# Where the edge features meet their weights: in the last attention loop, or in four earlier ones

## The chip, the cores and the metric

The kernel runs on one core of a Trainium2 chip as one program. The time is the device time of that core in microseconds (us), the median of ten runs. The engines are named as in the profile: PE (matrix products, with PEld for loading weights), DVE (vector work), ACT (activations and copies), POOL (here almost only indirect DMAs: gathers and scatters of rows by an index), SP (here only starts DMAs). Each engine works through its own instructions in order.

## The reference

A graph of 3125 nodes with 256 features each and 50,000 edges sorted by destination goes through four layers; each layer is an attention over the edges and then a feed-forward part, each added to `x`. The third feed-forward part holds an attention of its own over another graph of 65,536 edges. Only the fourth attention uses the edges' own features:

```python
x = x + L0_gnn(norm(x), edge_index, ...);  x = x + L0_ffn(norm(x), ...)
x = x + L1_gnn(norm(x), edge_index, ...);  x = x + L1_ffn(norm(x), ...)
x = x + L2_gnn(norm(x), edge_index, ...);  x = x + L2_ffn(norm(x), other_edges, ...)
x = x + L3_gnn(norm(x), edge_index, edge_attr_256, ...);  x = x + L3_ffn(norm(x), ...)

def L3_gnn(x, edge_index, edge_attr, Wq, bq, Wk, bk, Wv, bv, We, Ws, bs):
    q, k, v = x @ Wq + bq, x @ Wk + bk, x @ Wv + bv       # 8 heads of 32
    e = edge_attr @ We                                    # 50000 x 256 by 256 x 256
    kj = k[src] + e
    alpha = segment_softmax(einsum("ehc,ehc->eh", q[dst], kj) / sqrt(32), dst)
    out = segment_sum((v[src] + e) * alpha, dst)
    return out + (x @ Ws + bs)
```

`L2_gnn` is two attentions, one after the other, so the graph is walked five times: g0, g1, g2a, g2b and, with edge features, g3. The product `e` depends on two inputs only and on nothing that the layers compute.

## The kernel before

**Edges.** The edges are split into 128 runs, one per partition, of T = 391 edges each; column `t` of a table holds the t-th edge of every run. Loops go over columns in groups of GW = 8, so each attention loop has 49 groups, the last with 7 columns. If the edges are not sorted (`L.wrong` > 0, not the case for this input) a counting sort makes the table, and `gnn3` first gathers the features into order (lines 838 to 844).

**The loops g0, g1, g2a, g2b** (`gat_once`, lines 592 to 613). Per group, POOL makes 8 gathers of 128 rows each into the tile `hg` (4 buffers); DVE adds the logits (line 607), runs two scans for the running maximum (645, 646) and subtracts (649); ACT takes the exponential `e` (652) and copies the maxima (653); DVE multiplies by `e` into a PSUM tile `v` in two halves (660) and adds the running sums column by column (668); SP stores the group, 1088 KB, to `OUT` (611). The order of DVE and ACT is that of the program text inside these loops (`manual_schedule`); PE, POOL and SP are ordered by the planner.

**After each loop**, `join_chunks` joins the 128 runs: PE turns the maxima (`mRT`, line 724), DVE scans them (729, 730), PE turns them back (733, 734), ACT takes an exponential `rs_` (739), DVE scales `R` (740), PE multiplies it (`carried`, 742); meanwhile POOL gathers `fixrow` from the stored rows (721); then ACT takes a second exponential (748), DVE mends the row and SP stores it (754). Only then can `node_results` gather the nodes' rows (`ng`).

**The sort of the second graph** (`sort_keys`, lines 289 to 347) belongs to the time of g0's loop: 14 of its stages go from DVE to PE (transposes), an ACT copy and back to DVE. The planner puts it between the groups.

**The loop in `ffn2`** (lines 1377 to 1417) has 8 steps. Each makes 64 gathers of 96-byte rows on POOL, computes up to six expert units on PE and ACT (28 in all, line 1348 on), starts one eighth of a copy of all edge features to a DRAM tile `attr` (`copy_features`, line 960, 6.25 MB a step), and then does one step of attention on DVE and ACT; `hg` has 3 buffers. The expert units store their results `y` to DRAM, 512 KB each (1370).

**The last attention loop** (`gnn3`, lines 889 to 942). Per group, POOL makes 16 gathers (8 rows `kv`, 8 rows `q`, 3 buffers each), SP loads 1 MB of `attr` into `at` (902), and `project` turns each pair of columns on PE (907), copies it on ACT (909) and multiplies it by `We` on PE into the PSUM tile `ape` (913), two pairs ahead. DVE adds `ape` to the keys and the values and multiplies by the queries (930, 932, 933), sums over each head (937), and goes on as in the other loops. `ffn3` follows.

Of the kernel before, what the change touches and what calls it, by code (L numbers as in the profile page):

```python
# [9 lines left out]
F32 = mybir.dt.float32  # L10
# [9 lines left out]
P = 128  # L20
C = 256
KC = C // P
N = 3125
NT = 25
NP = NT * P
# [3 lines left out]
GB = 64  # L29
GV = 4  # L30
# [8 lines left out]
class Kernel:  # L39
# [514 lines left out]
    def gat_once(self, L, tag, load_z, load_w, a_src, a_dst, H, dh, eps, loops, use):  # L554
# [4 lines left out]
        nc, tc, T, Ep = self.nc, self.tc, L.T, L.Ep  # L559
        Fh = H * dh  # L560
        W = Fh + H
# [4 lines left out]
        with tc.tile_pool(name=tag + "k", bufs=1) as kp:  # L566
# [25 lines left out]
            with tc.tile_pool(name=tag + "e", bufs=1) as sp, tc.tile_pool(name=tag + "v", bufs=4) as vp, \  # L592
                    tc.tile_pool(name=tag + "vp", bufs=2, space=PSUM) as pp, \
                    tc.manual_schedule(engines={mybir.EngineType.DVE, mybir.EngineType.Activation}):

                ad = sp.tile([P, T, L.zc], F32, name="ad")
                self.spread(L, D, ad, H, tag)
                rows = OUT[:Ep].rearrange("(p t) w -> p t w", p=P)
                carry = None
                for t in range(0, T, GW):  # L600
                    n = min(GW, T - t)
                    g = vp.tile([P, GW, RW], F32, name="hg")
                    for j in range(n):
                        self.gather(g[:, j, :], HT, L.tab[:, t + j, 0:1])
                    l = vp.tile([P, H, GW + 1], F32, name="l")
                    ln = l[:, :, 1 : n + 1]
                    nc.vector.tensor_tensor(
                        ln, g[:, :n, W:].rearrange("p n h -> p h n"), ad[:, t : t + n, :H].rearrange("p n h -> p h n"), ALU.add)
                    self.lrelu(ln, ln)
                    carry = self.weigh(L, carry, vp, pp, t, n, l, g, H, dh)  # L610
                    nc.sync.dma_start(out=rows[:, t : t + n, :], in_=g[:, :n, :])
                nc.vector.tensor_copy(R, carry[0])
                nc.vector.tensor_copy(mR, carry[1][:, :, 0])  # L613

# [9 lines left out]
    def weigh(self, L, carry, vp, pp, t, n, l, g, H, dh):  # L624
# [201 lines left out]

    def gnn3(self, L):

        nc, tc, a, T, Ep = self.nc, self.tc, self.a, L.T, L.Ep
        H, dh = 8, 32  # L830
        W = C + H
        RW = W + H
        Q = self.dram.tile([NP, C], F32, name="g3_Q")
        KV = self.dram.tile([NP, C + W], F32, name="g3_KV")
        OUT = self.dram.tile([Ep + 1 + P, RW], F32, name="g3_OUT")
        heads = lambda x: x.rearrange("p n (h d) -> p n h d", h=H)
        r = nc.values_load(L.wrong[0:1, 0:1], min_val=0, max_val=P)
        with tc.If(r > 0):
            with tc.tile_pool(name="g3s", bufs=3) as sp:
                rows = self.attr.rearrange("(p t) c -> p t c", p=P)  # L840
                for t in range(T):
                    x = sp.tile([P, C], F32, name="ax")
                    self.gather(x, a["edge_attr_256"], L.tab[:, t, 2:3])
                    nc.sync.dma_start(out=rows[:, t, :], in_=x)
# [37 lines left out]
        with tc.tile_pool(name="g3k", bufs=1) as kp:  # L882
            R = kp.tile([P, W], F32, name="R")
            mR = kp.tile([P, H], F32, name="mR")
            we = kp.tile([P, KC, C], F32, name="we")
            nc.sync.dma_start(out=we, in_=a["L3_gnn_We"].rearrange("(k p) f -> p k f", p=P))
            attr = self.attr.rearrange("(p t) c -> p t c", p=P)
            rows = OUT[:Ep].rearrange("(p t) w -> p t w", p=P)
            with tc.tile_pool(name="g3v", bufs=3) as vp, tc.tile_pool(name="g3vp", bufs=1, space=PSUM) as pp, \
# [4 lines left out]
                def project(i):  # L894

                    if i >= len(pairs):
                        return
                    t, j = pairs[i]
                    n = min(GW, T - t)
                    if j == 0:  # L900
                        at[t] = vp.tile([P, GW, C], F32, name="at", bufs=2)
                        nc.sync.dma_start(out=at[t][:, :n, :], in_=attr[:, t : t + n, :])
                    k2 = min(2, n - j)
                    pt = pp.tile([P, 2, KC, P], F32, name="apt")
                    for i2 in range(k2):
                        for k in range(KC):
                            nc.tensor.transpose(pt[:, i2, k, :], at[t][:, j + i2, k * P : (k + 1) * P], self.ident)  # L907
                    aT = vp.tile([P, 2, KC, P], F32, name="aT")
                    nc.scalar.copy(aT[:, :k2], pt[:, :k2])  # L909
                    pe = pp.tile([P, 2, C], F32, name="ape", bufs=2)  # L910
                    for i2 in range(k2):
                        for k in range(KC):
                            nc.tensor.matmul(pe[:, i2, :], aT[:, i2, k, :], we[:, k, :], start=(k == 0), stop=(k == KC - 1))  # L913
                    proj[i] = pe

                project(0)
                project(1)
                carry, i = None, 0
                for t in range(0, T, GW):
                    n = min(GW, T - t)  # L920
# [5 lines left out]
                    for j in range(0, n, 2):  # L926
                        k2 = min(2, n - j)
                        pe = proj.pop(i)
                        kj = pp.tile([P, 2, C], F32, name="kj")
                        nc.vector.tensor_tensor(kj[:, :k2], g[:, j : j + k2, :C], pe[:, :k2], ALU.add)  # L930
# [10 lines left out]
                nc.vector.tensor_copy(R, carry[0])  # L941
                nc.vector.tensor_copy(mR, carry[1][:, :, 0])

            self.join_chunks(L, "g3", OUT, R, mR, H, dh)
# [5 lines left out]
            self.node_results(L, "g3", OUT, H, dh, 1e-16, None, use)  # L950

    def copy_features(self, E, i, n):

        nc, tc = self.nc, self.tc
        src = self.a["edge_attr_256"]
        assert E % 16 == 0
        cut = lambda x: x.rearrange("(s r) c -> s r c", s=16)
        size = E // 16
        lo, hi = size * i // n, size * (i + 1) // n
        tc.keep_in_program_order(nc.sync.dma_start(out=cut(self.attr[:E])[:, lo:hi], in_=cut(src[:E])[:, lo:hi]))  # L960
        if i == 0:
            nc.sync.dma_start(out=self.attr[E:], in_=src[: self.attr.shape[0] - E])

# [327 lines left out]
    def ffn2(self, L):  # L1291
# [12 lines left out]
        with tc.tile_pool(name="f2", bufs=1) as sp:  # L1304
# [35 lines left out]
            with tc.tile_pool(name="f2e", bufs=1) as ep, tc.tile_pool(name="f2v", bufs=3) as vp, \  # L1340
# [7 lines left out]
                def expert(e, b0, n):  # L1348
# [9 lines left out]
                    for f in range(FC):  # L1358
# [1 line left out]
                        for k in range(KC):  # L1360
                            nc.tensor.matmul(ps[:, :n], w1[:, k, f * P : (f + 1) * P], zT[:, k, b0 : b0 + n], start=(k == 0), stop=(k == KC - 1))
                        nc.scalar.activation(hT[:, f, :n], ps[:, :n], AF.Gelu, bias=b1[:, e * FC + f : e * FC + f + 1])
                    y = wp.tile([P, 4, C], F32, name="y")
                    for i in range(n // P):
                        po = pp.tile([P, C], F32, name="ps2")
                        for f in range(FC):
                            nc.tensor.matmul(po, hT[:, f, i * P : (i + 1) * P], w2[:, f, :], start=(f == 0), stop=False)
                        nc.tensor.matmul(po, ones, b2[:, e, :], start=False, stop=True)
                        nc.scalar.copy(y[:, i, :], po)
# [7 lines left out]
                for i, t in enumerate(range(0, T, GB)):  # L1377
# [134 lines left out]
def tile_kernel(ctx: ExitStack, tc: tile.TileContext, a, out):  # L1512
    k = Kernel(tc, ctx, a, out)
    k.attr = k.dram.tile([(50000 + P - 1) // P * P, C], F32, name="attr")
    A = k.edges_by_destination("A", a["src"], a["dst"], 50000, 8)

    with tc.tile_pool(name="s4", bufs=1) as k.sort_pool, tc.tile_pool(name="sortp", bufs=1, space=PSUM) as k.sort_psum:
        k.gnn0(A)
# [30 lines left out]
```

## Time and profile before

| | us |
|---|---|
| median of 10 runs | 6276.6 (6273.5 to 6282.3) |
| the profiled execution | 6279.5 |
| its span, first to last instruction | 6277.4 |

| part | from to | us |
|---|---|---|
| loop g0, first gather to `R` | 149.0 to 665.8 | 517 |
| loop g1, end at `R` | 1939.7 | |
| loop g2a, first gather to `R` | 2319.8 to 2821.9 | 502 |
| loop g2b, first gather to last `R` | 2934.8 to 3434.0 | 499 |
| loop of ffn2, first gather to last store | 3572.1 to 4342.7 | 771 |
| loop g3, first gather to `R` | 4556.7 to 5577.5 | 1021 |

Over the whole span DVE is busy 56%, POOL 51%, PE 41%, ACT 13%. A row of the profile's groups reads: line, engine, operation, output tile <- input tiles, number of instructions | busy us, mean ns of one | idle time of that engine just before them, and what ended it ("issue" is time in which it waited for nothing that the profile shows). A row of the timeline reads: start, duration, engine, line, operation, tiles, and in brackets the idle time before it and what ended it. A row of the windows gives the busy time and the number of instructions of PE, PEld, DVE, ACT and POOL in a stretch, then the granted clock of PE as a share of full speed, the mean busy share of the 16 DMA engines, and GB/s.

### The profile page before, as it was taken

The numbers are of one execution on the slowest core, as the hardware profiler recorded it, in microseconds if no ns is written. First come the engines' busy times: TensorE is split into PE (matmuls) and PEld (weight loads), VectorE is DVE, ScalarE is ACT, GpSimd is POOL, SyncE is SP. The second block draws the span as 40 slices with busy tenths as digits, with TensorE's granted clock in tenths as the row PEclk, the third lists the DMA queues.
The fourth block names the chain that finished last, engine by engine and source line by source line (L and its number), as shares of the span: only waits on it lengthen the run. The fifth ranks groups of instructions, "written<-read, shape, count | busy, mean of one in ns | idle before, by whom it ended". The sixth has DMA issues, their size and how long they took to land. (4 is left out here: it accounts for less than half of the span.)

```text
span 6277.4 us, 39477 instructions
## 1 busy us (share of the span) xinstructions
PE 2590.0 (41%) x9265; PEld 1740.5 (28%) x9265; DVE 3503.0 (56%) x8011; ACT 794.1 (13%) x1810; POOL 3224.6 (51%) x3326
## 2 busy tenths in 40 slices
PE   2000049921001930002000599400566666639999
PEld 1000037710000620001000355200245555525555
DVE  6998611156886268884776411112778888871111
ACT  1000012210001110001000122100011111102222
POOL 3777430037774137765776576675077777740000
PEclk9555569955555975555555699755776666657999
DMA  5566335516663026663666134522377887730000
GB/s 192 189 226 222 124 113 169 157 57 198 224 219 109 14 66 225 224 217 111 210 211 205 46 103 126 157 55 69 142 257 263 263 269 261 262 122 16 10 11 26
DMA packets 398594, 963.74 MB, mean 154 GB/s; under 512 B 92478, under 2 KB 241053, under 8 KB 365966
## 3 DMA queue, kind: packets, MB, share of 16 engines
q1 hardware_dynamic: 236254, 538.71, 24.0%
q0 software_dynamic: 162096, 422.40, 23.9%
q8 instruction: 77, 1.26, 0.1%
q14 instruction: 167, 1.37, 0.1%
HBM read 611.38 MB, written 400.71 MB: 161 GB/s over the span
## 5 line engine op out<-in xcount | busy, mean ns | idle before, releaser
L724 PE MATMUL mRT<-ident,mR 128*8 128x128 f32 (+2 forms) x6 | 2.2, 373 | 2222.3 <-DVE mR L613 1352.2
L129 POOL DMA_INDIRECT hg<-g_H,A_tab x782 | 758.0, 969 | 238.9 <-issue 226.4
L668 DVE SCALAR_TENSOR_TENSOR hg<-hg,A_keep,v 128x264 f32<-128x264 f32 (+1 forms) x1368 | 666.2, 487 | 44.2
L129 POOL DMA_INDIRECT hg<-f_H,B_tab x512 | 516.0, 1008 | 239.0 <-issue 147.5
L724 PEld LDWEIGHTS mRT<-ident,mR 128*8 128x8 f32 (+2 forms) x6 | 0.5, 82 | 2224.9 <-issue 2224.9
L913 PE MATMUL ape<-we,aT 128*128 128x256 f32 x1564 | 492.0, 485 | 149.9 <-DVE kv L932 146.3
L129 POOL DMA_INDIRECT kv<-g_KV,A_tab x391 | 369.8, 946 | 295.7 <-issue 281.9
L660 DVE TENSOR_TENSOR v<-hg,e 128x1056 f32<-128x1056 f32 (+1 forms) x392 | 487.8, 1244 | 3.5 <-ACT e L652 3.5
L913 PEld LDWEIGHTS ape<-we,aT 128*128 128x128 f32 x1564 | 382.9, 251 | 249.5 <-DVE kv L932 163.3
L129 POOL DMA_INDIRECT hg<-g2a_H,A_tab x391 | 371.9, 951 | 119.1 <-issue 107.3
L129 POOL DMA_INDIRECT q<-g_Q,A_tab x391 | 369.7, 946 | 122.6 <-issue 105.7
L129 POOL DMA_INDIRECT hg<-g2b_H,A_tab x391 | 369.7, 945 | 119.1 <-issue 111.8
L1501 DVE SCALAR_TENSOR_TENSOR xs<-ps,g,xs 128x256 f32<-128x256 f32 x200 | 94.2, 484 | 457.4 <-PE ps L1500 457.4
L1386 DVE TENSOR_TENSOR l<-hg,ad 128x256 f32<-128x256 f32 x8 | 6.3, 790 | 610.1 <-DMA hg<-f_H,B_tab 610.1
L652 ACT ACTIVATE e<-d 128x72 f32<-128x72 f32 (+1 forms) x245 | 54.8, 224 | 2135.4 <-DVE d L649 2135.3
L125 PE MATMUL tr<-ident,z 128*128 128x128 f32 x450 | 111.0, 378 | 499.5 <-DVE z L117 435.8
L134 POOL DMA_INDIRECT A_Z<-D,A_first x100 | 99.2, 992 | 354.8 <-PE tr L125 316.2
L907 PE MATMUL apt<-ident,at 128*128 128x128 f32 x782 | 195.1, 385 | 197.7 <-ACT aT L909 189.1
L129 POOL DMA_INDIRECT y<-f_Y,pos x50 | 47.4, 948 | 397.6 <-DMA f_Y<-y 382.6
L125 PEld LDWEIGHTS tr<-ident,z 128*128 128x128 f32 x450 | 72.6, 203 | 537.0 <-ACT ln_rs L109 316.4
L1494 ACT ACTIVATE hT<-ps,bn 128x512 f32<-128x512 f32 (+1 forms) x224 | 162.4, 731 | 389.7 <-PE ps L1492 389.7
L930 DVE TENSOR_TENSOR kj<-kv,ape 128x512 f32<-128x512 f32 x196 | 135.8, 693 | 132.6 <-PE ape L913 117.4
(476 smaller groups left out, 6481.8 us busy)
## 6 DMA issues: line engine op xcount, KB each, us to landing
g_OUT<-hg SPq DMA_DIRECT2D x96, 1088.0 KB
g2a_OUT<-hg SPq DMA_DIRECT2D x48, 1088.0 KB
g_OUT<-kv SPq DMA_DIRECT2D x48, 1088.0 KB
g2b_OUT<-hg SPq DMA_DIRECT2D x48, 1032.0 KB
at<-attr SPq DMA_DIRECT2D x48, 1024.0 KB
w<-in_L_ffn_w_dram SPq DMA_DIRECT2D x80, 512.0 KB
attr<-in_edge_attr_dram SPq DMA_DIRECT2D x5, 6256.0 KB
attr<-in_edge_attr_dram SPq DMA_DIRECT2D x3, 6240.0 KB
```

Source lines behind the costliest of these rows:

```text
L125: nc.tensor.transpose(ps[:, k, :], z[:, t, k * P : (k + 1) * P], self.ident)
L129: return self.nc.gpsimd.indirect_dma_start(out=out, out_offset=None, in_=table, in_offset=bass.IndirectOffsetOnAxis(ap=idx, axis=0))
L134: i = self.nc.gpsimd.indirect_dma_start(out=table, out_offset=bass.IndirectOffsetOnAxis(ap=idx, axis=0), in_=in_, in_offset=None)
L652: nc.scalar.activation(e, d, AF.Exp)
L660: nc.vector.tensor_tensor(vals(v)[:, :k], vals(g[:, j0 : j0 + k, :W]), e[:, :, j0 + 1 : j0 + k + 1].rearrange("p h n -> p n h").unsqueeze( ...
L668: nc.vector.scalar_tensor_tensor(to, prev, L.keep[:, t + j0 + j : t + j0 + j + 1], v[:, j, :], op0=ALU.mult, op1=ALU.add)
L907: nc.tensor.transpose(pt[:, i2, k, :], at[t][:, j + i2, k * P : (k + 1) * P], self.ident)
L913: nc.tensor.matmul(pe[:, i2, :], aT[:, i2, k, :], we[:, k, :], start=(k == 0), stop=(k == KC - 1))
L930: nc.vector.tensor_tensor(kj[:, :k2], g[:, j : j + k2, :C], pe[:, :k2], ALU.add)
L1386: nc.vector.tensor_tensor(ln, g[:, :, W:].rearrange("p n h -> p h n"), ad[:, t : t + GB, :H].rearrange("p n h -> p h n"), ALU.add)
L1494: nc.scalar.activation(hT[:, f, :n], ps[:, :n], AF.Relu, bias=bn[l][1][:, c0 : c0 + 1], scale=bn[l][0][:, c0 : c0 + 1])
L1501: nc.vector.scalar_tensor_tensor(self.xs[:, t, :], po, g[:, t, e : e + 1], self.xs[:, t, :], op0=ALU.mult, op1=ALU.add)
```

## The change

The copy of the features in `ffn2` goes away. Instead each of the 196 groups of g0, g1, g2a and g2b calls `features`, which moves one pair of columns through four stages, one stage per call: load the pair's features (256 KB, and two rows of 1 KB for the last partition); turn them on PE; copy the turned pair on ACT and multiply it by `We` on PE; copy the product on ACT and store it (256 KB) to `attr`. `end_features` empties the stages at the end of each loop. `v` in `weigh` has one buffer instead of two. The weights are loaded once, into a tile that stays.

`gnn3` then loads the products from `attr`, and in place of the transposes and products each pair is copied by ACT from `at` to the PSUM tile `ape`, three pairs ahead. All of `gnn3` now stands twice in the program, in the two ways of a branch: one for unsorted edges (features gathered, and multiplied there) and one for sorted edges (`Else`, which this input takes). In `ffn2` the results `y` are stored in halves (256 KB, 3 buffers).

```diff
@@ gat_once, at the end of each group and of the loop
                     nc.sync.dma_start(out=rows[:, t : t + n, :], in_=g[:, :n, :])
+                    self.features(vp, pp)
+                self.end_features(vp, pp)
@@ weigh
-            v = pp.tile([P, GV, W], F32, name="v")
+            v = pp.tile([P, GV, W], F32, name="v", bufs=1)
@@ gnn3
+        r = self.nc.values_load(L.wrong[0:1, 0:1], min_val=0, max_val=P)
+        with self.tc.If(r > 0) as way:
+            self.gnn3_edges(L, False)
+        with way.Else():
+            self.gnn3_edges(L, True)
...
                     k2 = min(2, n - j)
+                    if ordered:
+                        proj[i] = pp.tile([P, 2, C], F32, name="ape", bufs=3)
+                        nc.scalar.copy(proj[i][:, :k2], at[t][:, j : j + k2, :])
+                        return
...
-                project(0)
-                project(1)
+                ahead = 3 if ordered else 2
+                for i in range(ahead):
+                    project(i)
...
-                        project(i + 2)
+                        project(i + ahead)
@@ new
+    def features(self, sp, pp, last=False):
...
+        rows = self.attr.rearrange("(p t) c -> p t c", p=P)
+        loaded, turned, made = f["stages"]
+        if made is not None:
+            (t, n), pe = made
+            o = sp.tile([P, 2, C], F32, name="fe_o", bufs=2)
+            nc.scalar.copy(o[:, :n], pe[:, :n])
+            nc.sync.dma_start(out=rows[:, t : t + n, :], in_=o[:, :n])
+            made = None
+        if turned is not None:
+            (t, n), pt = turned
+            aT = sp.tile([P, 2, KC, P], F32, name="fe_T", bufs=2)
+            nc.scalar.copy(aT[:, :n], pt[:, :n])
+            pe = pp.tile([P, 2, C], F32, name="fe_p", bufs=1)
+            for i in range(n):
+                for k in range(KC):
+                    nc.tensor.matmul(pe[:, i, :], aT[:, i, k, :], self.feat_we[:, k, :], start=(k == 0), stop=(k == KC - 1))
+            made, turned = ((t, n), pe), None
+        if loaded is not None:
+            (t, n), at = loaded
+            pt = pp.tile([P, 2, KC, P], F32, name="fe_t", bufs=1)
+            for i in range(n):
+                for k in range(KC):
+                    nc.tensor.transpose(pt[:, i, k, :], at[:, i, k * P : (k + 1) * P], self.ident)
+            turned, loaded = ((t, n), pt), None
+        if not last and f["at"] < len(f["units"]):
+            t, n = f["units"][f["at"]]
+            f["at"] += 1
+            at = sp.tile([P, 2, C], F32, name="fe_a", bufs=3)
+            whole = src[: full * T].rearrange("(p t) c -> p t c", t=T)
+            nc.sync.dma_start(out=at[:full, :n, :], in_=whole[:, t : t + n, :])
+            for i in range(n):
+                at_end = full * T + t + i
+                nc.sync.dma_start(out=at[full:, i, :], in_=src[min(at_end, E - 1) : min(at_end, E - 1) + 1])
+            loaded = (t, n), at
+        f["stages"] = [loaded, turned, made]
+
+    def end_features(self, sp, pp):
+        while any(x is not None for x in self.feat["stages"]):
+            self.features(sp, pp, last=True)
@@ ffn2
-                    y = wp.tile([P, 4, C], F32, name="y")
                     for i in range(n // P):
+                        if i % 2 == 0:
+                            y = wp.tile([P, 2, C], F32, name="y", bufs=3)
...
-                    nc.sync.dma_start(out=Y[b0 : b0 + n, e, :].rearrange("(i p) c -> p i c", p=P), in_=y[:, : n // P, :])
+                        if i % 2 or i == n // P - 1:
+                            at = b0 + i // 2 * 2 * P
+                            nc.sync.dma_start(out=Y[at : b0 + (i + 1) * P, e, :].rearrange("(i p) c -> p i c", p=P), in_=y[:, : i % 2 + 1, :])
...
-                    self.copy_features(50000, i, T // GB)
```

More of the change, by code (lines that the diff above doesn't have):

```diff
@@ L827, in gnn3, with gnn3_edges @@
     def gnn3(self, L):
+        r = self.nc.values_load(L.wrong[0:1, 0:1], min_val=0, max_val=P)
[3 more added lines that the diff above has]
+            self.gnn3_edges(L, True)
+    def gnn3_edges(self, L, ordered):
         nc, tc, a, T, Ep = self.nc, self.tc, self.a, L.T, L.Ep
@@ L832, in gnn3 @@
         RW = W + H
-        Q = self.dram.tile([NP, C], F32, name="g3_Q")
-        KV = self.dram.tile([NP, C + W], F32, name="g3_KV")
-        OUT = self.dram.tile([Ep + 1 + P, RW], F32, name="g3_OUT")
+        way = "g3o" if ordered else "g3"
+        Q = self.dram.tile([NP, C], F32, name=way + "_Q")
+        KV = self.dram.tile([NP, C + W], F32, name=way + "_KV")
+        OUT = self.dram.tile([Ep + 1 + P, RW], F32, name=way + "_OUT")
         heads = lambda x: x.rearrange("p n (h d) -> p n h d", h=H)
[L837 to L844, printed above, removed]
         with tc.tile_pool(name="g3t", bufs=1) as sp, tc.tile_pool(name="g3tp", bufs=2, space=PSUM) as pp:
@@ L884, in gnn3 @@
             mR = kp.tile([P, H], F32, name="mR")
-            we = kp.tile([P, KC, C], F32, name="we")
-            nc.sync.dma_start(out=we, in_=a["L3_gnn_We"].rearrange("(k p) f -> p k f", p=P))
             attr = self.attr.rearrange("(p t) c -> p t c", p=P)
@@ L901, in project @@
                         at[t] = vp.tile([P, GW, C], F32, name="at", bufs=2)
-                        nc.sync.dma_start(out=at[t][:, :n, :], in_=attr[:, t : t + n, :])
+                        if ordered:
+                            nc.sync.dma_start(out=at[t][:, :n, :], in_=attr[:, t : t + n, :])
+                        else:
+                            for i2 in range(n):
+                                self.gather(at[t][:, i2, :], a["edge_attr_256"], L.tab[:, t + i2, 2:3])
                     k2 = min(2, n - j)
+                    if ordered:
+                        proj[i] = pp.tile([P, 2, C], F32, name="ape", bufs=3)
+                        nc.scalar.copy(proj[i][:, :k2], at[t][:, j : j + k2, :])
+                        return
                     pt = pp.tile([P, 2, KC, P], F32, name="apt")
@@ L912, in project @@
                         for k in range(KC):
-                            nc.tensor.matmul(pe[:, i2, :], aT[:, i2, k, :], we[:, k, :], start=(k == 0), stop=(k == KC - 1))
+                            nc.tensor.matmul(pe[:, i2, :], aT[:, i2, k, :], self.feat_we[:, k, :], start=(k == 0), stop=(k == KC - 1))
                     proj[i] = pe
-                project(0)
-                project(1)
+                ahead = 3 if ordered else 2
+                for i in range(ahead):
+                    project(i)
                 carry, i = None, 0
@@ L942, in gnn3 @@
                 nc.vector.tensor_copy(mR, carry[1][:, :, 0])
-            self.join_chunks(L, "g3", OUT, R, mR, H, dh)
+            self.join_chunks(L, way, OUT, R, mR, H, dh)
             def use(t, n, v, pool):
@@ L948, in use @@
                 nc.vector.tensor_tensor(x, x, v, ALU.add)
-            self.node_results(L, "g3", OUT, H, dh, 1e-16, None, use)
-    def copy_features(self, E, i, n):
-        nc, tc = self.nc, self.tc
-        src = self.a["edge_attr_256"]
[L956 to L962, printed above, removed]
+            self.node_results(L, way, OUT, H, dh, 1e-16, None, use)
@@ new lines, in start_features @@
+    def start_features(self, E, T):
+        self.feat = dict(E=E, T=T, units=[(t, min(2, T - t)) for t in range(0, T, 2)], at=0, stages=[None] * 3)
+        self.feat_we = self.const.tile([P, KC, C], F32, name="feat_we")
+        self.nc.sync.dma_start(out=self.feat_we, in_=self.a["L3_gnn_We"].rearrange("(k p) f -> p k f", p=P))
+        self.feat_pool = None
+    def features(self, sp, pp, last=False):
+        nc, f = self.nc, self.feat
+        E, T = f["E"], f["T"]
+        full, rest = divmod(E, T)
+        src = self.a["edge_attr_256"]
+        rows = self.attr.rearrange("(p t) c -> p t c", p=P)
[33 more added lines that the diff above has]
+        f["stages"] = [loaded, turned, made]
@@ L1368, in expert @@
                         nc.tensor.matmul(po, ones, b2[:, e, :], start=False, stop=True)
-                        nc.scalar.copy(y[:, i, :], po)
-                    nc.sync.dma_start(out=Y[b0 : b0 + n, e, :].rearrange("(i p) c -> p i c", p=P), in_=y[:, : n // P, :])
+                        nc.scalar.copy(y[:, i % 2, :], po)
+                        if i % 2 or i == n // P - 1:
+                            at = b0 + i // 2 * 2 * P
+                            nc.sync.dma_start(out=Y[at : b0 + (i + 1) * P, e, :].rearrange("(i p) c -> p i c", p=P), in_=y[:, : i % 2 + 1, :])
                 outr = OUT[:Ep].rearrange("(p t) w -> p t w", p=P)
@@ L1515, in tile_kernel @@
     A = k.edges_by_destination("A", a["src"], a["dst"], 50000, 8)
+    k.start_features(50000, A.T)
     with tc.tile_pool(name="s4", bufs=1) as k.sort_pool, tc.tile_pool(name="sortp", bufs=1, space=PSUM) as k.sort_psum:
```

## The prediction, made before the changed kernel ran

> **What bounds the kernel now.** I read the windows of the attention loops first, because the change puts work into four of them and takes work out of two.
>
> ```profile
> 149.00:670.00 521.00, 16.41 (x60) 10.83 (x61) 460.36 (x1070) 32.49 (x114) 386.87 (x392) 0.50 0.65 213
> 1438.00:1945.00 507.00, 1.97 (x5) 0.87 (x5) 406.23 (x850) 27.59 (x100) 373.19 (x393) 0.50 0.66 218
> ...
> 3572.00:4345.00 773.00, 419.98 (x1431) 249.38 (x1429) 113.89 (x251) 119.70 (x225) 515.96 (x512) 0.78 0.39 105
> 4556.00:5577.00 1021.00, 665.63 (x2346) 510.66 (x2346) 853.02 (x1371) 133.94 (x295) 739.51 (x782) 0.68 0.78 256
> ```
>
> Rows: g0, g1, ffn2, g3. In g1 PE and ACT are idle; POOL is busy 373 of 507 us. That is POOL at its limit: a gather takes 0.95 us and the next starts 0.30 us later, so a group of 8 takes 10.0 us and 49 take 490. In g3 782 gathers at 1.25 us are 977 us; the first starts at 4556.7, the last at 5540.2, 983.5 us later. So POOL sets the pace there too, although DVE is busy 84%. Next, the groups with all that ended their waits:
>
> ```profile
> L129 POOL DMA_INDIRECT hg<-f_H,B_tab x512 | 516.0, 1008 | 239.0 <-issue 147.5 <-DMA hg<-f_H,B_tab 91.2 <-ACT hT L1362 0.3
> ...
> L930 DVE TENSOR_TENSOR kj<-kv,ape 128x512 f32<-128x512 f32 x195 | 135.3, 694 | 132.6 <-PE ape L913 117.4 <-DMA kv<-g_KV,A_tab 10.6
> ```
>
> In ffn2 POOL waits 239.0 us before 512 gathers. At 0.305 each 156 would do; 83 are left, and they are waits for earlier gathers to land. POOL's and SP's timeline of one step shows where:
>
> ```profile
> 4150.25 0.56 SPq L960 DMA_DIRECT2D attr<-in_edge_attr_dram  x1
> ...
> 4159.01 0.95 POOL L129 DMA_INDIRECT hg<-f_H,B_tab  x1 [0.30 <-issue]
> 4162.49 0.94 POOL L129 DMA_INDIRECT hg<-f_H,B_tab  x1 [2.53 <-DMA hg<-f_H,B_tab]
> 4167.37 0.94 POOL L129 DMA_INDIRECT hg<-f_H,B_tab  x1 [3.94 <-DMA hg<-f_H,B_tab]
> 4173.30 0.94 POOL L129 DMA_INDIRECT hg<-f_H,B_tab  x1 [4.99 <-DMA hg<-f_H,B_tab]
> 4175.34 0.94 POOL L129 DMA_INDIRECT hg<-f_H,B_tab  x1 [1.10 <-DMA hg<-f_H,B_tab]
> ```
>
> The feature copy starts at 4150.25, and the gathers behind it stall for 11.4 us beyond the usual 0.30. All eight steps show this (7.2 to 12.8 us), the four last ones with no expert work left. The 32.7 us by which the 512 gathers themselves are longer (1008 ns against 944) fall on DVE's lines 1405 and 1415 and stay.
>
> The end of a loop (g2a) on ACT, PE and SP:
>
> ```profile
> 2815.76 0.29 ACT L653 COPY hg<-m 128x56 f32<-128x56 f32 x1
> ...
> 2822.39 0.37 PE L724 MATMUL mRT<-ident,mR 128*8 128x128 f32 x1 [511.92 <-issue]
> ...
> 2824.86 0.21 ACT L739 ACTIVATE rs__17567<-rs__17567 128x8 f32<-128x8 f32 x1 [8.82 <-DVE rs__17567 L738]
> ...
> 2831.19 0.32 SPq L754 DMA_DIRECT2D g2a_OUT<-fixrow  x1
> ```
>
> **Part 1, the copy leaves ffn2: -83.** POOL would make its last gather 83 us sooner. What takes over? The 28 expert units end at about 4000 and are bound by PE (99% busy until 3970): six a step are 91 us, 28 are done near 3997, while POOL at (638 + 33)/8 = 84 us a step ends at 4243. So POOL still ends last, and DVE's 17 us behind it stay. The stores of `y` in halves are 52 instead of 28; the six 512 KB stores of the first step cost POOL nothing visible beyond 1.4 us, and ACT's copies wait at most for a store three halves back. Bounds -70 to -88.
>
> **Part 2, g3: -16.** The products of g3 leave PE; ACT has as many copies as before, and 1 MB is loaded per group as before. In the loop POOL is the limit, so most of DVE's 117.4 us of waiting for `ape` is not on the path. What is gained is DVE's lag at the end.
>
> ```profile
> 5540.21 0.94 POOL L129 DMA_INDIRECT kv<-g_KV,A_tab  x1 [0.30 <-issue]
> ...
> 5564.66 0.70 DVE L930 TENSOR_TENSOR kj<-kv,ape 128x512 f32<-128x512 f32 x1 [1.30 <-PE ape L913]
> ...
> 5577.50 0.30 DVE L941 COPY R<-kv 128x264 f32<-128x264 f32 x1
> ```
>
> DVE ends 37 us after the last gather's start, as its group takes 20.4 us (18.0 without 117.4/49 = 2.4). Without that lag: the last gather of the group before the last starts ten gathers earlier, 5527.7, and lands 4.6 us later (median of `kv`). From its last pair DVE needs 12.6 us (5546.96 to 5559.5): 5544.9. Three pairs of 1.96 of the last group follow, 5550.7, then 10.9 us from its single column to `R` (5566.63 to 5577.5): 5561.6. That is 16 sooner. Bounds -5 (DVE still late behind ACT's new copies) to -21 (only landing and 10.9 us).
>
> **Part 3, the work in the four loops.** A call adds, per 10 us: on PE four transposes (1.1 us) and eight product instructions, 3.7 us at g3's slowest (12 in 5.49 us at 5560.84) or 1.89 at its fastest (5016.16); on ACT two copies of 0.58; on SP four more DMAs of 0.3 to 0.45 us. PE and ACT are idle there, and each product has a full group until the next stage, so ACT's `e`, behind the two copies, isn't late (its idle time before `e` is 9.4 us). In the built order SP's loads stand three groups ahead of their use; before a load SP waits for the transposes of three calls back, about 8 us into the group, 2 before the next store is due. With four buffers a late store costs nothing. `v` with one buffer: g3 has it already, and there its second half starts 3.38 us after the first instead of 3.27; 0.1 to 0.2 us of DVE's 1.1 idle per group. The DMA engines: 538.71 MB on SP's queue took 24.0% of 16 x 6277 us, 44.7 engine-us per MB; 0.52 MB per group is 23 engine-us, 1.5 us on each of 16, so their share goes from 0.66 to 0.81. At 0.78 in g3 POOL kept 1.259 us per gather against 1.249. I take 1 us per loop, +4 (0 to +25).
>
> The Trainium skill's page "DMA: Bandwidth & Descriptors" speaks against this part (section "Bandwidth"): transfers should be 1 MiB or more, and one costs 2.0 us plus its bytes over 436 GB/s. An estimate by it: two of 256 KB are 5.2 us, on top of 6.6 us of a group's 10 already taken, 1.8 us too much, 353 us over 196 groups. The g3 row, 256 GB/s at 0.78 with no loss, weighs more.
>
> **Part 4, the ends of the loops: +17.** In the built order ACT does seven copies between the last `m` copy and `rs_`, and PE's `mRT` stands behind the last products: copy, copy, products, transposes, copy, products, transposes, copy, products, copy. From 2816.05 that is 1.2 + 3.7 + 1.1 + 0.6 + 3.7 + 1.1 + 0.6 + 3.7 + 0.6, 2832.3, against 2822.4 before. `mRT` to the end of `R` is 3.1 us, `carried` and two DVE steps 2.4: SP's store would be issued near 2838.0, 6.8 late (3.1 us of the delay lie under the wait for `fixrow`, landed at 2829.2). With fast products and transposes it is 0.3. PE's clock in these loops is 0.50, so I take 5 for three loops, and 2 for g2b, where `fixrow` lands 3.2 us later behind weight loads: +17 (1 to 27).
>
> The page "TensorE: Matmul & The Clock Gate" (Part 1) says that PE runs at half clock until about 3.4 us of sustained work. If each call's burst were enough, the fast price would hold and this term would be 1; no row of these loops shows PE at work.
>
> **Part 5, g0's sort: +6.** Until about 370 us DVE is full: 18 groups begin 11.3 us apart, POOL's gathers 10.0, and at 376.8 POOL first waits for a buffer. So DVE's further delay there is POOL's. `v` adds 18 x 0.2 = 4. The sort's 14 turns share PE and ACT with `features` (busy 4.8 of 11 us): 14 x 0.44 x 2.4 = 15 at most; the planner puts other DVE work in between, I take 2. Bounds 0 to +20.
>
> **Part 6, the branch: +6.** At the branch before g3 DVE now stands still 1.02 us; at the first branch of the program, past 1382 DVE instructions as it will be past 1324 here, 4.44. That is up to +3.4, and about 1 for the jump behind g3. Seven of the 25 `ln_st` of ffn3 now run between gathers and cannot cross it: 7 x 0.39 = 2.7. I take 6 (3 to 9).
>
> **Sum.** -83 - 16 + 4 + 17 + 6 + 6 = -66. From the span of 6277.4: 6211; the profiled execution took 6279.5, the median is 6276.6, 0.8 below the span, so about 6211 as a median.
>
> **Rivals.** *The stall moves with the bytes (slower).* The copy cost 83 us for 50 MB; the same 50 MB now pass through the four loops, where POOL is the limit too. At the same price they give back 83: about 6294. It decides from 66/196 = 0.34 us per group. For it: the share 0.81, above any row, and g2a's gathers already land after 4.9 us. Against: g3 moves as much in pieces of 1 MB and loses 7 us in all; the stall needs gathers as late as those behind a copy of 6.25 MB.
> *The stall isn't the copy's alone.* If half of the 83 us belonged to the steps' own stores and weight loads: 6252. Against: the last steps have neither expert stores nor weights and stall longest.
> *The ends and the sort cost their upper bounds*: +10, +14 and the branch +3: 6238.
> *All at their lower bounds*: -88 - 21 + 0 + 1 + 0 + 3 = -105: 6172. PE warm and `features` wholly hidden speak for it.
> *The change doesn't do what it says*: were the unsorted way taken, 391 more gathers of 1.25 us in g3 would add 489 us; the present trace has no gather on line 843, so the edges are sorted. I give it nothing.
>
> **The numbers.** Forecast 0.62 (6188 to 6236), stall with the bytes 0.13, half the stall 0.09, upper bounds 0.11, lower 0.05. The time is 6211, the range 6180 to 6258. About 0.2%, 12.6 us, is what a measurement here can tell from no change: faster 0.84, within 0.04, slower 0.12.
>
> **What would show it.** Right: ffn2's loop near 690 us with no wait for landed gathers; the four loops' gathers still 1.25 us apart; 5 us more from the last `e` to the store of `fixrow`; g3's `R` about 21 us after the last gather; DMA share near 0.8 in g1. Wrong: waits "DMA hg" on POOL in g1 or g2a, ACT's `e` late behind `fe_T`, or POOL waiting for DVE through much of g0.

## The result and the profile after

The changed kernel takes 7431.4 us (median of 8 runs, 7427.4 to 7434.5), the one before 6276.6 (28 runs): a ratio of 1.184 (95% interval 1.183 to 1.185), 1155 us slower, where 66 less was forecast. The kernel before itself took 6269 us beside e5 and e6 and 7103 to 7195 us beside all other runs below, for a reason that wasn't found, so each run is set only against the kernel before measured with it, and the groups are compared by the median of their periods, which stays near 10 us for the kernel before there too (10.08 in e15, 10.00 in the first trace). The profiled execution has a span of 7425.7 us, 1148.3 more than before. First its windows, of the loops g1, ffn2 and g3 (first gather to `R` or to the last store), with the columns of the windows of before.

```profile
1762.00:2560.00 798.00, 209.79 (x568) 156.57 (x568) 408.55 (x844) 70.47 (x192) 372.46 (x392) 0.58 0.48 167
...
4812.00:5502.00 690.00, 413.29 (x1405) 244.99 (x1403) 113.09 (x249) 119.97 (x223) 517.04 (x513) 0.80 0.21 43
5719.00:6716.00 997.00, 0.00 (x0) 0.00 (x0) 849.41 (x1363) 142.16 (x295) 740.34 (x782) 0.50 0.81 261
```

ffn2 and g3 became shorter, as forecast. g1, first gather to `R`, went from 502 us to 795 with the same busy time of POOL (372 us) and of DVE (409, before 406): new waiting, not new work. The mean share of the DMA engines, which should have gone from 0.66 to 0.81, fell to 0.48. Where the span went, by the starts of POOL's gathers in the two traces:

| stretch | before | after | |
|---|---|---|---|
| first to last gather of g0 | 505.7 | 804.6 | +298.9 |
| of g1 | 491.1 | 781.5 | +290.4 |
| of g2a | 491.0 | 786.2 | +295.2 |
| of g2b | 488.7 | 770.7 | +282.0 |
| last gather to the first gather of `ng`, the four together | 94.6 | 153.3 | +58.7 |
| first to last gather of ffn2 | 753.8 | 671.5 | -82.3 |
| first gather of g3 to `fixrow` | 1025.8 | 1008.9 | -16.9 |
| the two stretches around g3 that the branch touches (from `ng` of ffn2 to g3; from the last `ng` to the end) | 827.0 | 832.3 | +5.4 |
| all else, nearly all of it ahead of the four loops' first gathers | | | +17 |

The groups with all that ended their waits: POOL in g2a, before and then after, POOL in ffn2, and DVE's `kj` in g3 (line 940 here):

```profile
L129 POOL DMA_INDIRECT hg<-g2a_H,A_tab x391 | 371.9, 951 | 119.1 <-issue 107.3
...
L129 POOL DMA_INDIRECT hg<-g2a_H,A_tab x391 | 372.0, 951 | 420.2 <-DVE d L651 274.4 <-issue 105.4 <-DVE m L648 13.4
...
L129 POOL DMA_INDIRECT hg<-f_H,B_tab x512 | 516.7, 1009 | 156.0 <-issue 155.7 <-DMA hg<-f_H,B_tab 0.3
...
L940 DVE TENSOR_TENSOR kj<-kv,ape 128x512 f32<-128x512 f32 x195 | 135.3, 694 | 106.1 <-DMA kv<-g3o_KV,A_tab 100.5 <-ACT ape L911 0.4
```

In ffn2 the 83 us of waits for landed gathers are gone; 156 us are 512 times the usual 0.305. In g3 DVE no longer waits for `ape`, only for its gathers. In g2a POOL's idle time grew from 119.1 us to 420.2, by 301. "DVE d" is only the last thing that happened before POOL went on; the timelines of SP, DVE and POOL show what it waited for.

```profile
3301.11 0.35 SPq L611 DMA_DIRECT2D g2a_OUT<-hg  x1
3301.55 0.37 SPq L984 DMA_DIRECT2D attr<-fe_o  x1
3302.02 0.38 SPq L1007 DMA_DIRECT2D fe_a<-in_edge_attr_dram  x1
3302.45 14.97 SPq L1010 DMA_DIRECT2D fe_a<-in_edge_attr_dram  x2
3317.79 0.35 SPq L611 DMA_DIRECT2D g2a_OUT<-hg  x1
```

```profile
3286.88 2.06 DVE L670 SCALAR_TENSOR_TENSOR hg<-hg,A_keep,v 128x264 f32<-128x264 f32 x4
```

```profile
3307.36 0.95 POOL L129 DMA_INDIRECT hg<-g2a_H,A_tab  x1 [0.30 <-issue]
3315.36 0.94 POOL L129 DMA_INDIRECT hg<-g2a_H,A_tab  x1 [7.05 <-DVE d L651]
...
3324.11 0.94 POOL L129 DMA_INDIRECT hg<-g2a_H,A_tab  x1 [0.30 <-issue]
3332.11 0.94 POOL L129 DMA_INDIRECT hg<-g2a_H,A_tab  x1 [7.07 <-DVE d L651]
```

A group takes 16.75 us: 10 us of gathers, 7 of waiting. SP spends 15 of them on two loads of 1 KB, directly behind the load of 254 KB, and the next store of `hg` is issued only then. The store issued at 3301.11 is the loop's 20th; DVE had finished its tile at 3288.94 (3286.88 + 2.06), so the store stood ready for 12.2 us. POOL's gather at 3315.36 is the first of the 24th group, which takes the same one of four buffers. So POOL waits for that store, 14.3 us from its issue.

The trace's records of single DMA packets (start, duration and size) say why. A store of `hg` has 128 packets of 8704 bytes. In g2a of the kernel before all 128 run within 2.9 to 4.0 us. In the changed kernel 120 run together within some 3 us, and 8, a sixteenth, start about 9 us after the first of them. One DMA engine out of 16 is late, and the load is what holds it: 127 packets of 2048 bytes, one after another, 80 ns apart, never two at once. The trace's records of completions agree: the semaphore of each of g2a's 49 stores receives 16 updates, the last of them 8.9 us (median) behind the fifteenth; that of each of the 196 loads receives two, one at its issue and one 26 us later (median); in e5 that of each of the 171 loads of 128 partitions receives 16. In the loop's steady state that engine has per group 127 x 0.080 = 10.2 us of the load, 16 gather packets of 0.22 (3.5), 8 of the store at 0.335 (2.7) and 8 of the products' store at 0.09 (0.7): 17.1 us, against a group of 16.75. The other 15 engines have 6.9. That is theory A of the experiments: the load of 127 partitions runs on one DMA engine.

The Trainium skill states the rule for it, on the page "DMA: Bandwidth & Descriptors", section "Why a DMA increments its semaphore by 16 and not by 1": a transfer runs on the largest number of engines up to 16 that divides the slowest dimension of both its sides, and 127 partitions put all on one. The packets above and those of the runs below agree with it.

### The profile page after: what moved, and what is told of

It reads as the page before. It is cut to its first block, busy times and chain, and to the rows that moved or that the text cites. A ratio compares the mean times of both kernels' runs of the same rounds, so it can differ in the third digit from the quotient of the medians.

```text
span 7425.7 us, 41109 instructions
## 1 busy us (share of the span) xinstructions
PE 2776.4 (37%) x9265; PEld 1862.1 (25%) x9265; DVE 3523.3 (47%) x8011; ACT 988.8 (13%) x2202; POOL 3219.7 (43%) x3326
## 5 line engine op out<-in xcount | busy, mean ns | idle before, releaser
L993 PE MATMUL fe_p<-feat_we,fe_T 128*128 128x256 f32 x1564 | 727.1, 645 | 2273.0 <-ACT fe_T L989 2272.9
L993 PEld LDWEIGHTS fe_p<-feat_we,fe_T 128*128 128x128 f32 x1564 | 489.4, 328 | 2442.7 <-ACT fe_T L989 2338.7
L607 DVE TENSOR_TENSOR l<-hg,ad 128x64 f32<-128x64 f32 (+2 forms) x196 | 48.7, 249 | 1292.5 <-DMA hg<-g_H,A_tab 563.1
L129 POOL DMA_INDIRECT hg<-g2a_H,A_tab x391 | 372.0, 951 | 420.2 <-DVE d L651 274.4
L129 POOL DMA_INDIRECT kv<-g3o_KV,A_tab x391 | 370.2, 947 | 295.8 <-issue 282.4
L129 POOL DMA_INDIRECT q<-g3o_Q,A_tab x391 | 370.1, 947 | 120.0 <-issue 107.2
L911 ACT COPY ape<-at 128x512 f32<-128x512 f32 x196 | 115.2, 588 | 755.1 <-DVE kv L942 671.3
L1000 PE MATMUL fe_t<-ident,fe_a 128*128 128x128 f32 x782 | 181.4, 378 | 67.5 <-DMA fe_a<-in_edge_attr_dram 50.1
```

The source lines that it names most:

```text
L129: return self.nc.gpsimd.indirect_dma_start(out=out, out_offset=None, in_=table, in_offset=bass.IndirectOffsetOnAxis(ap=idx, axis=0))
L911: nc.scalar.copy(proj[i][:, :k2], at[t][:, j : j + k2, :])
L993: nc.tensor.matmul(pe[:, i, :], aT[:, i, k, :], self.feat_we[:, k, :], start=(k == 0), stop=(k == KC - 1))
L1000: nc.tensor.transpose(pt[:, i, k, :], at[:, i, k * P : (k + 1) * P], self.ident)
```

## The experiments

Rivals to theory A: B, the number of SP's transfers, each of which waits for the one eight places before it (the trace shows eight semaphores used in turn); C, the one-row loads; D, the new work on PE and ACT or the store; E, the bytes of the loads. A period is the time from a group's first gather to the next group's, here in g2a. Outside e5 and e6 the means of the periods are longer than the medians (11.4 us for the kernel before in e15, 11.7 in e1, 12.5 in e2, 12.4 in e3, 12.3 in e4, against 16.2 in the changed kernel of the first trace): they set e1 to e4 apart from the changed kernel, but only the medians set e3 apart from e2 and e4. The totals expected of e1 to e4 were set against the first trace; they were not met and prove nothing either way.

**e1, no load.** `at = self.feat_we` in place of the tile and its three loads.

> Leaves out the loads of the edge features in the four attention loops (the 127-partition load and both one-row loads); the transposes read the weights' tile instead, so the products are of other numbers. Transposes, copies, products and the store of 256 KB per group stay. Theory A (one DMA engine): in the changed kernel's packet records the 127 packets of 2 KB of a load come one after another, 80 ns apart, 10.2 us; with one engine's sixteenth of the group's gathers (16 x 0.22 = 3.5 us), of the group's 1 MB store (8 x 0.335 = 2.7) and of the product store (8 x 0.09 = 0.7) that is 17.1 us, against a group of 16.75 us. Without the load the groups go back to 10.0 us and the time to 6180 to 6230 us. Rival B (five transfers from SP per group, each waiting for the eighth before it): two are left, so 10.0 us too, 6180 to 6230. Rival C (the one-row loads, whose issue holds SP's queue 14 us): 6180 to 6230 too. Rival D (PE's and ACT's new work or the product store holds the group): the groups stay above 14 us and the time above 7000 us.

7113.6 us beside 7148.2. A group of g2a: median 10.1 us. D falls: with all of PE's, ACT's and the store's work half of the groups take what POOL's gathers take.

**e2, 112 and 15 partitions.**

```diff
-nc.sync.dma_start(out=at[:full, :n, :], in_=whole[:, t : t + n, :])
+nc.sync.dma_start(out=at[:112, :n, :], in_=whole[:112, t : t + n, :])
+nc.sync.dma_start(out=at[112:full, :n, :], in_=whole[112:, t : t + n, :])
```

> The load of 127 partitions is made as two, of 112 and of 15 partitions; the same bytes, both one-row loads kept, one transfer from SP more per group (six instead of five). Theory A: 112 partitions go over 16 engines (7 packets each) and 15 over 15 (1 each), so no engine has more than 0.64 us of the load; one engine then has 3.5 + 2.7 + 0.7 + 0.6 = 7.5 us of work per group, less than POOL's 10.0, and the time falls to 6190 to 6250 us. Rival B (number of transfers): six per group instead of five, 16.75 x 6/5 = 20 us per group, about 8070 us. Rival C (one-row loads): nothing changes, 7430 us. Rival E (the 50 MB of loads themselves, whatever engine carries them): 7430 us.

7214.6 us beside 7148.2, 1.010 (1.008 to 1.012). Group of g2a: median 10.04. B, C and E fall together: more transfers, the same one-row loads, the same bytes, and the median is back, where B forecast 20 us and C and E 16.75. Against B there is also the trace of the changed kernel: the transfer eight places before the first of the two one-row loads at 3302.45 had landed at 3297.83, so their 14.97 us aren't a wait for it. The issue of a one-row load now takes 0.25 us (median, at most 1.5), in the changed kernel 2.4 (at most 20.0).

**e3, 122 and 5 partitions**, the same edit with 122.

> The load is made as two of 122 and of 5 partitions. 122 has 2 as its largest divisor up to 16, 5 has 5. Theory A, with the count of engines as the largest divisor: 61 packets of 2 KB on each of two engines, 61 x 0.08 = 4.9 us, and with 3.5 + 2.7 + 0.7 + 0.1 us for the rest 11.9 us per group (11.6 if scaled by 16.75/17.1): 196 groups 1.6 to 1.9 us longer than 10.0, so 6500 to 6600 us. Were the partitions dealt out evenly whatever their number (only 127 being a special case): 6190 to 6250 us. Rival B: 20 us per group, 8070. Rival C: 7430.

7271.1 us beside 7148.2. Group of g2a: median 11.3. POOL's timeline of e3, first gathers of six groups in a row:

```profile
2836.13 0.95 POOL L129 DMA_INDIRECT hg<-g2a_H,A_tab  x1 [1.92 <-DVE hg L670]
2847.21 0.94 POOL L129 DMA_INDIRECT hg<-g2a_H,A_tab  x1 [1.36 <-DMA g2a_OUT<-hg]
2858.42 0.95 POOL L129 DMA_INDIRECT hg<-g2a_H,A_tab  x1 [1.50 <-DVE hg L670]
2869.69 0.94 POOL L129 DMA_INDIRECT hg<-g2a_H,A_tab  x1 [1.56 <-issue]
2881.12 0.95 POOL L129 DMA_INDIRECT hg<-g2a_H,A_tab  x1 [1.72 <-issue]
2892.02 0.95 POOL L129 DMA_INDIRECT hg<-g2a_H,A_tab  x1 [1.19 <-issue]
```

They are 10.9 to 11.4 us apart, and before each POOL waits 1.2 to 1.9 us; one row names the store of `hg`, the others DVE or nothing (part of this trace's records of completions is missing, so such names are unsure). The periods lie between the 10.0 of 16 engines and the 16.75 of one, a little under the 11.6 expected of two. An even deal of partitions would have given 10.0. In e3 the one-row loads are issued in 0.27 us (median, at most 2.2), so SP's queue is not what makes its groups longer; that speaks for the work of the busiest engines as the limit. No semaphore of a load of 122 partitions receives more than three updates, and of 5 no more than six, one of them at the issue: two engines and five. The first load of g0 in each run shows the number of engines without the rest, from the packet records:

```
packets of the first load                          first start to last end    most at once
127 partitions (after; e6)                          11.63; 10.90 us            1
122 of 122 + 5 (e3, e9, e12, e14, e16)              5.95 to 6.82               2
112 of 112 + 15 (e2; e8)                            1.41; 1.27                 15; 16
128 partitions (e4; e5)                             1.52; 1.46                 16; 15
```

**e4, 128 partitions.**

```diff
+if t + n <= E - full * T:
+    nc.sync.dma_start(
+        out=at[:, :n, :],
+        in_=bass.AP(tensor=src.tensor, offset=src.offset + t * C, ap=[[T * C, P], [C, n], [1, C]]))
+else:
+    nc.sync.dma_start(out=at[:112, :n, :], in_=whole[:112, t : t + n, :])
+    nc.sync.dma_start(out=at[112:full, :n, :], in_=whole[112:, t : t + n, :])
...
```

> For the 171 pairs of columns where the last partition has whole rows, one load of 128 partitions, no one-row loads (three transfers from SP per group); for the 25 pairs behind them 112 + 15 partitions and the one-row loads as before. It computes the same. Theory A: 8 packets per engine, 0.64 us; the groups are POOL's 10.0 us and the time is 6180 to 6240 us, a little under the run with 112 + 15 if SP's six transfers cost anything there. Rival B: 16.75 x 3/5 = 10.05 us, about 6220 too. Rival C: 6200 to 6250. Rival E (bytes): 7430.

7206.7 us beside 7148.2, 1.008 (1.007 to 1.010); group of g2a: median 10.04. The median is as theory A says; the total can't be set beside the first trace, so the same kernel was measured again, next to the changed one.

> The kernel of the run with loads of 128 partitions once more, because on the chip of the first four runs the kernel before itself took 7148 us instead of 6277, so that their times can't be set beside the first trace. If the kernel before takes about 6277 us here: theory A (one DMA engine carries the 127-partition load) gives groups of 10.0 us in the four loops and 6180 to 6240 us; rival E (the bytes of the loads, on whatever engine) 7430. If the kernel before takes about 7150 here too, 1.005 to 1.012 of it, as in the first runs.

> The changed kernel as it is, beside the run with loads of 128 partitions on one chip. If the kernel before takes about 6277 us here: 7425 to 7435 us, groups of 16.75 us. If it takes about 7150 us: theory A has one engine's 16.75 us per group as the limit on this chip as well, so the four loops stay near 780 us each while the rest grows as the kernel before does: 7.9 to 8.3 thousand us.

The kernel before took 6269.3 us here (7 runs). e5: **6196.5 us, 0.988 of it (0.986 to 0.990)**. e6, the changed kernel: 7429.7 (one run). Nothing differs but how the same features are loaded: 1233 us, and groups of g2a of 10.00 us (median) against 16.74. The windows of g1 and the groups of POOL in e5:

```profile
1447.00:1955.00 508.00, 212.32 (x583) 158.24 (x584) 409.04 (x844) 72.33 (x196) 373.64 (x393) 0.61 0.80 267
```

```profile
L129 POOL DMA_INDIRECT hg<-g2a_H,A_tab x391 | 372.2, 952 | 119.1 <-issue 108.8 <-DVE hg L670 8.2 <-DMA hg<-g2a_H,A_tab 2.1
```

The DMA share is 0.80, where 0.81 was forecast, at 267 GB/s, and POOL's idle time is 119.1 us again, its usual 0.30 per gather. SP's timeline of a group in e5, where no issue takes longer than 0.33 us:

```profile
2506.46 0.33 SPq L1008 DMA_DIRECT2D fe_a<-in_edge_attr_dram  x1
2508.02 0.32 SPq L611 DMA_DIRECT2D g2a_OUT<-hg  x1
2511.51 0.32 SPq L984 DMA_DIRECT2D attr<-fe_o  x1
```

**The repeats e7 to e9, e11, e12, e14, e16** were to give the totals beside a kernel before of 6270 us, and none did.

> The kernel without the loads of the edge features once more (the transposes read the weights' tile, so the products are of other numbers), beside a kernel before that takes about 6270 us. The run with loads of 128 partitions took 6196.5. Theory A (the load, through its one engine): the same 6180 to 6200 us, groups of 10.0 us. Rival D (PE's and ACT's new work or the product store): above 7000.

> The load as two of 112 and 15 partitions, the one-row loads kept, six transfers from SP per group. Theory A: 6190 to 6230 us. Rival B (the number of transfers from SP, each waiting for the eighth before it): 16.75 x 6/5 = 20 us per group, above 8000. Rival C (the one-row loads): 7430.

> The load as two of 122 and 5 partitions. Theory A with the largest divisor up to 16 as the number of engines (122: 2; 5: 5): one engine then has 61 x 0.08 = 4.9 us of the load and 7.0 of the rest, 11.6 to 11.9 us per group, 6500 to 6600 us. Dealt out evenly whatever the number: 6190 to 6250. Rival C: 7430.

> The load as two of 112 and 15 partitions, the one-row loads kept, once more, because in both earlier runs of it the kernel before took over 7100 us. If it takes about 6270 here: theory A 6190 to 6230 us; rival B (number of transfers from SP) above 8000; rival C (the one-row loads) 7430.

> The load as two of 122 and 5 partitions, once more for the same reason. If the kernel before takes about 6270 us: theory A with the largest divisor up to 16 as the number of engines (2 for 122) 11.6 to 11.9 us per group, 6500 to 6600 us; dealt out evenly whatever the number 6190 to 6250; rival C 7430.

> The load as two of 122 and 5 partitions. In the earlier runs of it half of the groups took 11.3 us or more in the third loop, against 10.04 with 112 and 15 partitions, but the kernel before took over 7100 us there. If it takes about 6270 us here: theory A (2 engines for 122 partitions) 11.2 to 11.9 us per group in three loops and 6410 to 6570 us; dealt out evenly whatever the number 6190 to 6250.

> The load as two of 122 and 5 partitions beside it. If the kernel before takes about 6270 us: theory A (2 engines for 122 partitions) 11.2 to 11.9 us per group in three loops and 6410 to 6570 us; dealt out evenly whatever the number 6190 to 6250. Otherwise groups with a median of 11.2 to 11.6 us as before.

Beside a kernel before of 7103.2: e7 7074.8, e8 7183.9 (1.011, 1.008 to 1.014), e9 7205.1. Beside 7194.7: e11 7248.9 (1.007, 1.005 to 1.010), e12 7309.1. Beside 7154.8: e14 7270.1; beside 7182.9: e16 7314.3. Group medians of g2a: 10.10 without load, 10.03 and 10.03 with 112 + 15, 11.26, 11.28, 11.32 and 11.20 with 122 + 5. The total with two engines beside a kernel before of 6270 us stays open: 6410 to 6570 was expected and not measured.

**e10 and e13, the kernel's own lists.** `src` and `dst` have always been loaded over 127 partitions. SP's timeline of the kernel before, at the start:

```profile
13.74 0.26 SPq L160 DMA_DIRECT2D dst<-in_dst_dram  x1
14.39 3.90 SPq L162 DMA_DIRECT2D dst<-in_dst_dram  x1
18.39 0.28 SPq L160 DMA_DIRECT2D src<-in_src_dram  x1
18.71 7.15 SPq L162 DMA_DIRECT2D src<-in_src_dram  x1
```

Here is the picture of the changed kernel, in small, before the change: a 127-partition load, and the one-row load behind it held for 3.9 and 7.15 us. The packets of the lists' 127-partition loads run one at a time, 8.2 us for the first 127. To e4 was added:

```diff
-nc.sync.dma_start(out=t[:full, :], in_=ap[: full * T].rearrange("(p t) -> p t", t=T))
+rows = ap[: full * T].rearrange("(p t) -> p t", t=T)
+cut = full // 16 * 16
+nc.sync.dma_start(out=t[:cut, :], in_=rows[:cut])
+nc.sync.dma_start(out=t[cut:full, :], in_=rows[cut:])
```

> The kernel with loads of 128 partitions, and the kernel's own two loads of 127 partitions (the lists src and dst at the start, 194 KB each, one engine's 127 packets of 1564 bytes in 8.4 us) made as 112 and 15 partitions too. In the trace of before VectorE waits 7.56 us for dst and 6.53 us for src. Theory A: both waits nearly go, and up to 14 us of the start with them if nothing else takes over: 6183 to 6192 us. If the start then waits for other loads behind them in SP's queue: 6190 to 6197, no change that can be told.

> Loads of 128 partitions in the attention loops, and the two lists at the start in 112 and 15 partitions. In the earlier run of it the first gather of the first loop began at 139.0 us, against 151.5 in the run with the lists left as they were, but the kernel before took over 7100 us there. If it takes about 6270 us here: theory A 6180 to 6188 us (6196.5 less 8 to 14), 0.985 to 0.987 of the kernel before.

e10: 7170.3 beside 7103.2, 1.010 (1.007 to 1.013). e13: 7195.0 beside 7154.8, 1.006 (1.004 to 1.008). Set against e4's 1.008, the totals show no gain. The waits of DVE in the first 60 us, of e5, of which the first two are missing in e10 and e13, while the third grows to 8.9 and 9.5 us:

```profile
DVE dst L163 <- DMA dst<-in_dst_dram: 7.7, 1, 7.7
DVE A_tab L166 <- DMA src<-in_src_dram: 6.5, 1, 6.5
DVE bjunk L412 <- DMA brow<-A_dst,at: 4.3, 3, 2.6
```

The first gather of the program starts at 37.7 (e10) and 37.5 (e13) instead of 51.0 (e4), g0's first at 139.0 and 141.4 instead of 151.5: 10 to 12.5 us, within the up to 14 expected. Taken off e5's 6196.5 that would be some 6185 us, an estimate from these differences; it was not measured.

**e15, the kernel before once more.**

> The kernel before, profiled in the same call as the next run. If it takes about 6270 us nothing is new in it: groups of 10.0 us, the eight steps of ffn2 as in the trace of before. If it takes over 7100 us, its profile shows which stages are longer in such a call; theory: engines pause between instructions that wait for nothing, in all stages with many small instructions, and the stages' shares are those of the run with 128 partitions (four loops near 580 us each instead of 491, ffn2 near 1050 instead of 754, g3 near 1150 instead of 984).

7158.4 us. Its four loops take 553 to 560 us from first to last gather, ffn2 1035, g3 1242, where near 580, 1050 and 1150 were expected. In e4, measured at another time, they are 595 to 601, 1014 and 1152. A line of DVE's waits in e4 shows pauses, 195 of up to 1.2 us behind its own instruction before (e5 has no such row):

```profile
DVE hg L670 <- DVE hg L670: 127.5, 195, 1.2
```

Part of the records of completions is missing in e4 too (13 of g2a's 49 stores show all 16), so the row shows idle time, but not surely what ended it. From first to last gather e4 is shorter than e15 in g3 and 35 to 46 us longer in each of the four loops, where e5 and the first trace differ by 0.3 to 0.7 us in g1, g2a and g2b. With loads of 128 partitions the change is 1.2% faster in e5 and 0.8% slower in e4, each against its own kernel before. What makes the pauses, whether they hold all engines, and why the added work is dearer there, wasn't found.

## Why the prediction was wrong

**The step that failed** is in part 3: "0.52 MB per group is 23 engine-us, 1.5 us on each of 16, so their share goes from 0.66 to 0.81." The 23 engine-us hold, but 10.2 us of them lie on one engine, so they are no 1.5 us on each of 16. By the sum of that step with the load on one engine, the engine's 17.1 us per group are 7.1 more than POOL's 10.0, and 196 groups 1390 us. Measured were 1166 from first to last gather: half of g2a's groups take 16.7 us or more, but their mean is 16.2, 6.15 more than the 10.07 before, and 48 such periods are the loop's 295. The diff shows `at[:full]` with `full` = 127, the trace of before has the price of it on SP's line 162, and neither was used. The same part took SP's four added DMAs at 0.3 to 0.45 us each; the two loads of 1 KB among them took 15 us together. The sentence "With four buffers a late store costs nothing." holds for a store late once, not for one that makes POOL wait 7 us in every group.

The other steps, measured in e5, where only the loads of the features differ from the changed kernel (128 partitions and no one-row loads in 171 of the 196 groups), against the first trace of the kernel before:

| step | forecast | e5 against before | |
|---|---|---|---|
| copy leaves ffn2 | -83 (-70 to -88) | -82.3 | the waits are gone; `y` in halves wasn't tested apart |
| g3's tail | -16 (-5 to -21) | -19.2 | 5.5 in the loop, 13.7 behind it |
| contention, g1, g2a, g2b | +1 each | +0.3, +0.3, +0.7 | at a DMA share of 0.80 |
| contention and sort in g0 | +7 | +6.1 | |
| ends of the four loops | +17 (1 to 27) | +7.7 | from the last gather to `ng` |
| branch | +6 (3 to 9) | +4.2 | 1.2 ahead of g3, 3.0 behind |

Their sum is -82.2, the whole span -81.2; against the kernel before measured beside it e5 gains 72.8 us. So the other terms came out near their sizes, the ends 9 us too dear, and -66 would have been 7 off for a kernel with loads of 128 partitions; the kernel of the diff is another. PE and SP at the end of g2a in e5 show what part 4 said:

```profile
2841.45 1.99 PE L993 MATMUL fe_p<-feat_we,fe_T 128*128 128x256 f32 x8 [0.73 <-ACT fe_T L989]
...
2844.16 0.27 PE L726 MATMUL mRT<-ident,mR 128*8 128x128 f32 x1 [0.72 <-ACT fe_o L983]
...
2849.38 0.32 SPq L756 DMA_DIRECT2D g2a_OUT<-fixrow  x1
```

`mRT` stands behind the last products as forecast; the store of `fixrow` comes 24.7 us after the last gather, before 20.4: 4.3 instead of 5. Of the three bursts of products behind the last exponential the first two took the slow 3.78 us, the third the fast 1.99. The ends of g0 and g1, up to `ng`, grew by 3.1 and 2.1, and that of g2b, for which 2 were taken, became 1.9 shorter.

**The rivals.** "The stall moves with the bytes" named the right place (POOL in the four loops) and a wait for a transfer to land, but not the mechanism: e5 moves the same bytes at a share of 0.80 and in g1, g2a and g2b it loses under 0.02 us per group instead of 0.34. The prediction weighed two rules of the skill. The estimate of 353 us from small transfers isn't borne out by e5, which uses transfers of the same 256 KB; the page has its price per transfer in the section "Anatomy of one DMA — SWDGE (gpsimd) path", fitted to transfers that GpSimd issues, and these are SP's. The rule on PE's clock agrees with the bursts as far as they go: in e5 nearly all bursts, some 10 us apart, took 3.78 us, and the third of three close together took 1.99. The rule that mattered, on the number of engines, stands on the first of these pages; the prediction didn't apply it to 127 partitions.

**The signs named beforehand.** ffn2's loop near 690 us: it is 688, with and without the 127 partitions. `R` of g3 21 us after the last gather: 23.1. A DMA share near 0.8 in g1: 0.48, and 0.80 in e5. Waits of POOL in g1 and g2a were named as the sign of an error, and they are there, though the profile puts them down to DVE.

## What to carry to other kernels

Before costing a transfer by its bytes, look at the first dimension of its access pattern: 127 partitions cost 80 ns per partition of 2 KB on one engine, 128 an eighth of it (1.46 us against 11.63), and 112 + 15 do as well where 128 don't exist. A mean share of 16 DMA engines can fall while one of them has become the bound; a small transfer whose issue takes many us, right behind a larger one on the same queue, was its sign here. A wait that the profile puts down to an engine that had nothing to do with the buffer is to be followed to the buffer's last user, here a store issued 14 us earlier and ready 12 us before that.

## What the runs showed of the hardware that was not expected

A load whose packets run one at a time delayed a sixteenth of a store that runs beside it: 8 of its 128 packets started some 9 us after the others. The issuing queue was held too: the two loads of 1 KB behind it took 15 us of SP's time per group, against 0.25 us each (median) once the same bytes went as 112 and 15 partitions (e2).
